# Attention scores on the four column quarters of the array, and VectorE to turn them back to pixels

## The chip, the cores and the metric

The kernel runs on one core of one Trainium2 chip. The metric is the device time of one execution in microseconds (us); the median over several runs counts. A core has TensorE (PE in the profile, with PEld for its weight loads), VectorE (DVE), ScalarE (ACT), GpSimd (POOL) and SyncE (SP), which run their own instruction streams and meet at semaphores. All data are fp32, and a fp32 matmul shows as two weight loads and two MATMUL instructions in the trace; a transpose by the identity shows as one of each.

## The reference

Two layers follow each other on x of shape (4, 64, 256, 256). The first is a transformer block with channel attention, a gated convolution and a patch-wise Fourier filter; the change does not touch it. The second, cut to what matters:

```python
def _lin_attn(x, wq, bq, wk, bk, wv, bv, wo, bo):      # x: (b, r, c, 64), 4 heads, one q and one k per head
    q = (x @ wq.T + bq).reshape(b_, r_, c_, H, DQK).swapaxes(2, 3)
    k = (x @ wk.T + bk).reshape(b_, r_, c_, H, DQK).swapaxes(2, 3)
    ...
    q = jax.nn.elu(q) + 1.0
    k = jax.nn.elu(k) + 1.0
    q = q / q.mean(axis=3, keepdims=True)
    k = k / k.sum(axis=3, keepdims=True)
    ktv = jnp.einsum('brhcd,brhce->brhde', k, v)
    o = jnp.einsum('brhcd,brhde->brhce', q, ktv)
    ...
xe = jnp.moveaxis(x, 1, -1)
h = xe + _lin_attn(_ln(xe, rn_g, rn_b), row_wq, row_bq, row_wk, ...)          # along rows
hc = _ln(h.swapaxes(1, 2), cn_g, cn_b)
h = h + _lin_attn(hc, col_wq, col_bq, col_wk, ...).swapaxes(1, 2)             # along columns
f = _ln(h, fn_g, fn_b)
f = jax.nn.gelu(f @ w1.T + b1, approximate=False) @ w2.T + b2
return jnp.moveaxis(h + f, -1, 1)
```

So each pixel has eight scores, four q and four k: a projection of its 64 channels by a 64x8 matrix, scaled by the pixel's reciprocal standard deviation, with a bias added.

## The kernel before

The program is a row of stages with HBM buffers between them. The first layer takes up to about 5390 us. **Stage c3** (to about 7300 us) ends the first layer (output projection and Fourier filter) and does the row attention of the second. **Stage d** (to the end) does the column attention and the feed-forward part. The change lies in these two.

**Stage c3** walks over 64 slabs: 2 pairs of images, 32 slabs of 8 rows each. Two images share a tile: 128 partitions by 16 blocks by 128 channels (two images of 64). Five generators work on different slabs at the same time, each one slab further behind: `product` (L938, output projection and transposes into zs), `patches` (L961, filter by matmuls L973 and L983, residual into xe at L986, layer-norm statistics), `features` (L1002), `attend` (L1039) and `update` (L1078). `_steps` calls them in turn, and each runs to its next `yield`.

`features` holds the projection. For each of four k, four blocks of xe are transposed on TensorE into one PSUM bank (L1009), ScalarE copies the bank to xrT (L1011), and four matmuls (L1014) project a block of 128 pixels each. The block is the stationary operand, 128x128, the weights rw (128x16, both images' 64x8 blocks) are the moving operand, and the result lies with pixels on partitions, 16 columns per block:

```python
for i in range(4):
    j = 4 * k + i
    T.matmul(qk[:, j * 16:(j + 1) * 16], xT[:, i * 128:(i + 1) * 128], rw, start=True, stop=True)
```

VectorE then scales (u, L1017), adds the bias (L1018), forms elu + 1 with ScalarE's Exp (`feature`, L672; f, L1021), and lays the scores out as kx (VectorE, L1028) and qx (GpSimd, L1029). `attend` multiplies kx into xe (L1046), `update` multiplies the mixed weights bdm into the pixels (L1085) and adds xe (h1, L1087).

**Stage d** walks over 32 iterations: 4 images, 8 groups of 32 columns. A tile h has 128 partitions (half of the 256 rows), 32 columns, two row halves and 64 channels. `attn` (L1157) of one group and `ffn` (L1248) of the group before it alternate through `_steps`. In `attn`, for each of 8 r, four columns are transposed (L1167), copied to xT by ScalarE (L1169) and projected by four matmuls (L1173) of the same form as L1014, with cwt in the place of rw; `spread` (L1139) takes the statistics of 16 channels' rows at a time. All 32 columns fill one bank qk of [128, 512]. Then u (L1176, L1177), fe, f (L1186) and kz (L1189) follow, and the products with h (L1195). `ffn` has the transposes L1255, the copy xfT (L1257), the first matmuls L1268, Gelu on ScalarE (L1270), and the second matmuls L1279 with the result st (L1281).

PSUM is split into six banks named mm and two named sm (`mm()` and `sm()`, L257 and L260). qk is an sm bank, and so are the products zp (c3) and the sums qs (d).

The source order gives the framework's scheduler a priority. The order of the instructions on each engine, and the buffers' turns, are planned by the scheduler with its own costs, so the order in the trace is not the order of the source.

Of the kernel before, what the change touches and what calls it, by code (L numbers as in the profile page):

```python
# [9 lines left out]
F32 = mybir.dt.float32  # L10
AF = mybir.ActivationFunctionType
ALU = mybir.AluOpType
# [235 lines left out]
def kernel(ctx: ExitStack, tc: tile.TileContext, x, packs, fd, out, off):  # L248
# [11 lines left out]
    def sm():  # L260
        return ps.tile([128, 512], F32, tag="sm", name="sm", bufs=2)
# [33 lines left out]
    def bc(ap, n):  # L295

        return ap.unsqueeze(2).to_broadcast([ap.shape[0], ap.shape[1], n])

    def mid_bc(ap, n):

        return ap.unsqueeze(1).to_broadcast([ap.shape[0], n, ap.shape[1]])
# [599 lines left out]
    def stage_c3():  # L901
        NS = H // 8
        with ExitStack() as cs:
# [3 lines left out]
            t = mm()  # L907
# [5 lines left out]

            t = mm()
            T.matmul(t[:, :16], K("rcen2"), rwg, start=True, stop=True)
            rw = p1.tile([128, 16], F32, name="rw")
            V.tensor_copy(rw, t[:, :16])
            t = mm()
            T.matmul(t[:65, :256], K("rcen1"), rgg, start=True, stop=True)
            rgt = p1.tile([65, 256], F32, name="rgt")  # L920
# [81 lines left out]
            def features(pr, s):  # L1002

                xe, rs = xes[pr, s]
                qk = sm()
                for k in range(4):
                    t = mm()
                    for i in range(4):
                        T.transpose(t[:, i * 128:(i + 1) * 128], xe[:, 4 * k + i], ident)  # L1009
                    xT = p.tile([128, 512], F32, name="xrT")  # L1010
                    S.copy(xT, t)  # L1011
                    for i in range(4):
                        j = 4 * k + i
                        T.matmul(qk[:, j * 16:(j + 1) * 16], xT[:, i * 128:(i + 1) * 128], rw, start=True, stop=True)  # L1014
                    yield
                u = p.tile([128, 32, 8], F32, name="u", bufs=1)
                V.tensor_tensor(u, qk[:, :256].rearrange("p (a c) -> p a c", c=8), bc(rs, 8), ALU.mult)  # L1017
                V.tensor_tensor(u, u, mid_bc(rbq, 32), ALU.add)  # L1018
                e = feature(p, u, [128, 32, 8])
                f = p.tile([128, 32, 8], F32, name="f", bufs=1)  # L1020
                V.scalar_tensor_tensor(f, u, 1.0, e, ALU.add, ALU.max)  # L1021

                qx = p.tile([128, 32, 8, 4], F32, name="qx")
                kx = p.tile([128, 32, 8, 4], F32, name="kx")
                mk = rmask.unsqueeze(1).unsqueeze(3)
                kr = p.tile([128, 32, 4], F32, name="kr", bufs=1)
                V.tensor_tensor(kr, f[:, :, 4:8], bc(rs, 4), ALU.mult)
                V.tensor_tensor(kx, kr.unsqueeze(2).to_broadcast([128, 32, 8, 4]), mk.to_broadcast([128, 32, 8, 4]), ALU.mult)  # L1028
                G.tensor_tensor(qx, f[:, :, 0:4].unsqueeze(2).to_broadcast([128, 32, 8, 4]), mk.to_broadcast([128, 32, 8, 4]), ALU.mult)  # L1029
                fr = p.tile([128, 2, 8], F32, name="fr")  # L1030
                V.tensor_reduce(fr, f.rearrange("p (j b) h -> p b h j", b=2), AX.X, ALU.add)
                qj = p.tile([128, 2, 2, 8, 4], F32, name="qj")
                kj = p.tile([128, 2, 8, 4], F32, name="kj")
                for b in (0, 1):
                    V.tensor_tensor(kj[:, b], mid_bc(fr[:, b, 4:8], 8), bc(rmask, 4), ALU.mult)
                    V.tensor_tensor(qj[:, :, b], fr[:, b, 0:4].unsqueeze(1).unsqueeze(1).to_broadcast([128, 2, 8, 4]), mk.to_broadcast([128, 2, 8, 4]), ALU.mult)
                fes[pr, s] = qx, kx, qj, kj
# [67 lines left out]
    def stage_d():  # L1105
        with ExitStack() as cs:
# [4 lines left out]

            t = mm()
            T.matmul(t[:, :16], K("cen2"), cwg, start=True, stop=True)
            cwt = p1.tile([128, 16], F32, name="cwt")
            V.tensor_copy(cwt, t[:, :16])
# [40 lines left out]

            def attn(h, xfs):  # L1157

                qk = sm()
                v1 = p1.tile([128, 64], F32, name="v1")  # L1160
                for r in range(8):
                    if r % 2 == 0:
# [5 lines left out]
                    xT = p.tile([128, 512], F32, name="xT")  # L1168
                    S.copy(xT, t)  # L1169
                    yield  # L1170
                    for i in range(4):
                        c = r * 4 + i
                        T.matmul(qk[:, c * 16:(c + 1) * 16], xT[:, i * 128:(i + 1) * 128], cwt, start=True, stop=True)  # L1173
                rs = rstd(v1, 64)
                u = p1.tile([128, 64, 8], F32, name="u")
                V.tensor_tensor(u, qk.rearrange("p (a c) -> p a c", c=8), bc(rs, 8), ALU.mult)  # L1176
                V.tensor_tensor(u, u, mid_bc(cbq, 64), ALU.add)  # L1177
                yield
                e = feature(p1, u, [128, 64, 8])
                yield  # L1180
                f = p1.tile([128, 2, 2, 32, 4], F32, name="f")
                uv = u.rearrange("p (c r) k -> p r c k", r=2)
                ev = e.rearrange("p (c r) k -> p r c k", r=2)
# [143 lines left out]
```

## Time and profile before

| | us |
|---|---|
| median of 3 runs (9669.94 to 9686.45) | 9681.12 |
| the profiled execution's own time | 9679.41 |
| span of the profile | 9677.6 |
| one slab of c3 (from L1051 to L1051) | 28.97 |
| one iteration of d (from L1210 to L1210) | 71.7 |

The profile is one execution. A row such as "L1014 PE MATMUL sm<-rw,xrT 128*128 128x16 f32 x2048 | 274.1, 266 | 12.7" says: line, engine, operation, output tile and inputs, the part of the array in use (rows*columns), the shape of the moving operand, the count, the busy time in us, the mean ns of one, and the idle time of the engine just before. Matmuls overlap, so 2048 of 266 ns make 274 us of busy time. In a timeline, the square bracket behind a row is the engine's idle time before it and what ended the idle time.

### The profile page before, as it was taken

How to read it: one execution, taken by the hardware profiler on the slowest of the kernel's cores; microseconds unless marked ns; L12 is line 12 of the kernel's file. 1: busy time of each engine (PE TensorE's matmuls, PEld its weight loads, DVE VectorE, ACT ScalarE, POOL GpSimd, SP SyncE). 2: the span in 40 equal slices, each digit the busy share in tenths (PEclk: the TensorE clock that was granted, in tenths of full speed). 3: DMA queues.
4: the chain of work that ended last, by engine and by line, in shares of the span. 5: the costliest groups of instructions: out<-in, count | busy, mean ns of one | idle time of the engine just before them, and what ended most of it. 6: DMA issues, size and time to landing. Idle time of an engine off the chain costs nothing. (4 is left out here: it accounts for less than half of the span.)

```text
span 9677.6 us, 130500 instructions
## 1 busy us (share of the span) xinstructions
PE 8860.6 (92%) x51310; PEld 4971.4 (51%) x51310; DVE 6090.5 (63%) x8570; ACT 4599.0 (48%) x7332; POOL 1134.1 (12%) x1828
## 2 busy tenths in 40 slices
PE   8999999698888888999999999999998999899997
PEld 7877777344444443333333466666665444444443
DVE  6666665466666664222222588888886777777775
ACT  4455555444444443222222344444444666666665
POOL 0111111111111111000000011111110000000000
PEclk9999999799999999999999999999997999999998
DMA  6677776799999998888888644444432322322322
GB/s 146 143 174 176 169 172 163 220 344 333 340 332 334 338 341 307 298 297 298 297 296 297 202 142 143 148 145 144 147 107 52 70 61 44 70 61 47 68 61 44
DMA packets 1258452, 1831.36 MB, mean 189 GB/s; under 512 B 335600, under 2 KB 1040112, under 8 KB 1196656
## 3 DMA queue, kind: packets, MB, share of 16 engines
q1 hardware_dynamic: 1053296, 1034.32, 36.7%
q0 software_dynamic: 204544, 788.69, 24.7%
q8 instruction: 407, 6.67, 0.3%
q14 instruction: 205, 1.68, 0.1%
HBM read 967.34 MB, written 788.53 MB: 181 GB/s over the span
## 5 line engine op out<-in xcount | busy, mean ns | idle before, releaser
L895 DVE TENSOR_TENSOR y<-ge,mm 128x512 f32<-128x512 f32 (+1 forms) x640 | 406.0, 635 | 1225.8 <-ACT ge L894 1225.8
L862 PE MATMUL mm<-t,w 128*128 128x512 f32 (+1 forms) x2560 | 1094.1, 566 | 19.6 <-DMA t<-td 19.6
L894 ACT ACTIVATE ge<-mm 128x512 f32<-128x512 f32 (+1 forms) x640 | 354.6, 554 | 1253.8 <-PE mm L869 1253.8
L862 PEld LDWEIGHTS mm<-t,w 128*128 128x128 f32 x2560 | 456.3, 190 | 647.3 <-issue 437.0
L755 PE MATMUL mm<-gp,wc 128*64 128x510 f32 (+1 forms) x3072 | 701.9, 596 | 83.1 <-DVE xm L765 50.9
L1270 ACT ACTIVATE hg<-mm,b 128x512 f32<-128x512 f32 x1024 | 629.3, 687 | 299.6 <-PE mm L1268 298.1
L599 PEld LDWEIGHTS mm<-wqk,gp 128*128 128x128 f32 x6144 | 712.0, 192 | 71.2 <-issue 42.3
L599 PE MATMUL mm<-wqk,gp 128*128 128x128 f32 x6144 | 733.7, 276 | 0.0
L1279 PE MATMUL mm<-hg,pack_d 128*64 128x512 f32 x2048 | 590.9, 632 | 109.7 <-ACT hg L1270 109.7
L810 ACT COPY tb<-mm 128x512 f32<-128x512 f32 x512 | 299.8, 586 | 779.8 <-PE mm L804 779.7
L804 PE MATMUL mm<-xl,pack_c 64*128 64x512 f32 x2048 | 532.5, 617 | 132.7 <-DVE tb L808 127.7
L1268 PE MATMUL mm<-xfT,w 64*128 64x512 f32 x2048 | 621.4, 673 | 3.2 <-ACT xfT L1257 2.9
L869 PE MATMUL mm<-t,w 64*64 64x504 f32 (+1 forms) x5120 | 575.6, 556 | 0.0
L755 PEld LDWEIGHTS mm<-gp,wc 128*64 128x64 f32 x3072 | 277.1, 137 | 462.3 <-issue 331.2
L309 ACT ACTIVATE ln_sq<-xn 128x1024 f32<-128x1024 f32 x256 | 274.6, 1073 | 429.0 <-DVE xn L307 428.9
L1281 DVE TENSOR_SCALAR st<-mm,pack_d 128x512 f32<-128x512 f32 x256 | 278.8, 1089 | 212.6 <-PE mm L1279 212.6
L804 PEld LDWEIGHTS mm<-xl,pack_c 64*128 64x128 f32 x2048 | 216.2, 189 | 376.7 <-DVE tb L808 186.7
L311 DVE TENSOR_REDUCE ln_v<-ln_sq 128x16 f32<-128x1024 f32 x256 | 311.6, 1218 | 146.8 <-ACT ln_sq L309 146.8
L765 DVE SCALAR_TENSOR_TENSOR xm<-mm,bx,xs 128x256 f32<-128x256 f32 x512 | 212.2, 476 | 297.3 <-PE mm L759 297.3
L1146 ACT ACTIVATE ln_sq<-xc 128x1024 f32<-128x1024 f32 x256 | 268.8, 1057 | 224.6 <-DVE xc L1144 223.4
L1268 PEld LDWEIGHTS mm<-xfT,w 64*128 64x128 f32 x2048 | 219.2, 206 | 297.6 <-issue 146.9
L1147 DVE TENSOR_REDUCE v<-ln_sq 128x16 f32<-128x1024 f32 x256 | 307.2, 1211 | 91.7 <-ACT ln_sq L1146 91.6
(448 smaller groups left out, 16826.0 us busy)
## 6 DMA issues: line engine op xcount, KB each, us to landing
t<-td SPq DMA_DIRECT2D x256, 1152.0 KB, 10.0
td<-tb POOLq DMA_DIRECT2D x144, 1024.0 KB, 10.6
td<-tb POOLq DMA_DIRECT2D x288, 512.0 KB, 9.2
yd<-y POOLq DMA_DIRECT2D x128, 1152.0 KB, 10.1
ya<-yd SPq DMA_DIRECT2D x192, 512.0 KB, 5.8
xs<-in_x_dram SPq DMA_DIRECT2D x128, 512.0 KB, 6.7
projd<-pj POOLq DMA_DIRECT2D x256, 256.0 KB, 4.8
gp<-projd SPq DMA_DIRECT2D x128, 512.0 KB, 7.5
```

The source lines that it names most:

```text
L311: V.tensor_reduce(s2, sq, AX.X, ALU.add)
L599: T.matmul(qp[:, k * 128:(k + 1) * 128], gp[:, 2 * i + k // 2, at + dx:at + dx + 128], wqk[:, dx, :], start=(dx == 0), stop=(dx == 2))
L755: T.matmul(tv[i * 64:(i + 1) * 64, :, o], wc[2 * pr + i][:, dx, :], gps[i][:, 2 * r:2 * r + 2, i_], start=(dx == 1), stop=False, skip_grou ...
L804: T.matmul(t, inT[q, hf * 128:(hf + 1) * 128], xls[b // 2, s][q, :, 2 * y:2 * y + 2].rearrange("p f y t -> p f (y t)"), start=True, stop=True)
L862: T.matmul(t[:, :n], w[:, 0:128], x_[:, c, :], start=True, stop=False, skip_group_check=True)
L869: T.matmul(t[po:po + 64, :n].rearrange("p (n c) -> p n c", c=64)[:, :, o], w[q:q + 64, 128:192], x_[q:q + 64, c, i_], start=False, stop=Tr ...
L894: S.activation(ge[:, :n], ts[0][k][:, :n], AF.Gelu)
L895: V.tensor_tensor(y[:, c, :].rearrange("p n c -> p (n c)"), ge[:, :n], ts[1][k][:, :n], ALU.mult)
L1147: V.tensor_reduce(s2, sq, AX.X, ALU.add)
L1268: T.matmul(t, w1[rh * 64:(rh + 1) * 64, i * 128:(i + 1) * 128], xT[rh * 64:(rh + 1) * 64], start=True, stop=True)
L1270: S.activation(g, t, AF.Gelu, bias=b1[:, i:i + 1])
L1279: T.matmul(y[rh * 64:(rh + 1) * 64, :], w2[:, i, :], hg[i * 2 + rh], start=False, stop=(i == 1), skip_group_check=True)
```

## The change

The operands are exchanged. The weights, filled up with zeros to 32 columns, become the stationary operand, 128x32, and the pixels become the moving operand. Of each of four blocks of 128 pixels, pixels 32g to 32g+31 go to column quarter g of the array: one matmul per quarter moves 4 x 32 = 128 pixels, and its result lies on partitions 32g to 32g+31, with the scores on partitions and pixels along the row. A group is still four matmul calls. VectorE then transposes the 32x32 blocks of a whole bank of [128, 512] into qp in SBUF, and so brings the pixels back to partitions, with 32 columns per block, of which 16 are used. In c3 the bank is filled once in a slab and transposed once. In d only 16 columns of the image fit into a bank, so there are two banks and two transposes per iteration, after r = 3 and r = 7. u reads the used columns of qp in place of qk. In c3 it writes to the tile u as before; in d it works in place in qp.

```diff
+    def bc4(ap, m, n):
+        v = ap.rearrange("p (a m) -> p a m", m=m)
+        return v.unsqueeze(3).to_broadcast([v.shape[0], v.shape[1], m, n])
...
-            rw = p1.tile([128, 16], F32, name="rw")
-            V.tensor_copy(rw, t[:, :16])
+            rw = p1.tile([128, 32], F32, name="rw")
+            V.memset(rw, 0.0)
+            V.tensor_copy(rw[:, :16], t[:, :16])
...
-                    for i in range(4):
-                        j = 4 * k + i
-                        T.matmul(qk[:, j * 16:(j + 1) * 16], xT[:, i * 128:(i + 1) * 128], rw, start=True, stop=True)
-                    yield
+                    for g in range(4):
+                        T.matmul(qk[g * 32:(g + 1) * 32, k * 128:(k + 1) * 128], rw, xT.rearrange("p (j n) -> p j n", j=4)[:, :, g * 32:(g + 1) * 32],
+                                 start=True, stop=True)
+                    yield
+                qp = p.tile([128, 16, 32], F32, name="qp")
+                V.transpose(qp.rearrange("p j m -> p (j m)"), qk)
                 u = p.tile([128, 32, 8], F32, name="u", bufs=1)
-                V.tensor_tensor(u, qk[:, :256].rearrange("p (a c) -> p a c", c=8), bc(rs, 8), ALU.mult)
+                V.tensor_tensor(u.rearrange("p (j b) c -> p j b c", b=2), qp[:, :, 0:16].rearrange("p j (b c) -> p j b c", b=2),
+                                bc4(rs, 2, 8), ALU.mult)
...
-                qk = sm()
+                qp = p1.tile([128, 32, 32], F32, name="qp")
...
                     yield
-                    for i in range(4):
-                        c = r * 4 + i
-                        T.matmul(qk[:, c * 16:(c + 1) * 16], xT[:, i * 128:(i + 1) * 128], cwt, start=True, stop=True)
+                    if r % 4 == 0:
+                        qk = sm()
+                    for g in range(4):
+                        T.matmul(qk[g * 32:(g + 1) * 32, r % 4 * 128:r % 4 * 128 + 128], cwt, xT.rearrange("p (c n) -> p c n", c=4)[:, :, g * 32:(g + 1) * 32],
+                                 start=True, stop=True)
+                    if r % 4 == 3:
+                        V.transpose(qp[:, r // 4 * 16:r // 4 * 16 + 16].rearrange("p c m -> p (c m)"), qk)
                 rs = rstd(v1, 64)
-                u = p1.tile([128, 64, 8], F32, name="u")
-                V.tensor_tensor(u, qk.rearrange("p (a c) -> p a c", c=8), bc(rs, 8), ALU.mult)
-                V.tensor_tensor(u, u, mid_bc(cbq, 64), ALU.add)
+                u = qp[:, :, 0:16].rearrange("p c (r k) -> p c r k", r=2)
+                V.tensor_tensor(u, u, bc4(rs, 2, 8), ALU.mult)
+                V.tensor_tensor(u, u, cbq.unsqueeze(1).unsqueeze(1).to_broadcast([128, 32, 2, 8]), ALU.add)
```

cwt is widened in the same way as rw, and the views of u and e behind it follow the new shape [128, 32, 2, 8].

More of the change, by code (lines that the diff above doesn't have):

```diff
@@ L1113, in stage_d @@
             T.matmul(t[:, :16], K("cen2"), cwg, start=True, stop=True)
-            cwt = p1.tile([128, 16], F32, name="cwt")
-            V.tensor_copy(cwt, t[:, :16])
+            cwt = p1.tile([128, 32], F32, name="cwt")
+            V.memset(cwt, 0.0)
+            V.tensor_copy(cwt[:, :16], t[:, :16])
             t = mm()
@@ L1170, in attn @@
                     yield
-                    for i in range(4):
-                        c = r * 4 + i
-                        T.matmul(qk[:, c * 16:(c + 1) * 16], xT[:, i * 128:(i + 1) * 128], cwt, start=True, stop=True)
+                    if r % 4 == 0:
[5 more added lines that the diff above has]
+                        V.transpose(qp[:, r // 4 * 16:r // 4 * 16 + 16].rearrange("p c m -> p (c m)"), qk)
                 rs = rstd(v1, 64)
-                u = p1.tile([128, 64, 8], F32, name="u")
-                V.tensor_tensor(u, qk.rearrange("p (a c) -> p a c", c=8), bc(rs, 8), ALU.mult)
-                V.tensor_tensor(u, u, mid_bc(cbq, 64), ALU.add)
+                u = qp[:, :, 0:16].rearrange("p c (r k) -> p c r k", r=2)
+                V.tensor_tensor(u, u, bc4(rs, 2, 8), ALU.mult)
+                V.tensor_tensor(u, u, cbq.unsqueeze(1).unsqueeze(1).to_broadcast([128, 32, 2, 8]), ALU.add)
                 yield
-                e = feature(p1, u, [128, 64, 8])
+                e = feature(p1, u, [128, 32, 2, 8])
                 yield
                 f = p1.tile([128, 2, 2, 32, 4], F32, name="f")
-                uv = u.rearrange("p (c r) k -> p r c k", r=2)
-                ev = e.rearrange("p (c r) k -> p r c k", r=2)
+                uv = u.rearrange("p c r k -> p r c k")
+                ev = e.rearrange("p c r k -> p r c k")
                 for rh in (0, 1):
```

## The prediction

> **What bounds the kernel now.** I read first the shares of busy time and the two stretches that the change touches (windows over the trace): stage c3, 5450 to 7270 us, and stage d, 7300 to 9670 us. Columns: stretch, us, then busy us and instructions of PE, PEld, DVE, ACT, POOL, granted TensorE clock, DMA share, GB/s.
>
> ```profile
> PE 8860.6 (92%) x51310; PEld 4971.4 (51%) x51310; DVE 6090.5 (63%) x8570; ACT 4599.0 (48%) x7332; POOL 1134.1 (12%) x1828
> 5450.00:7270.00 1820.00, 1715.15 (x10841) 1111.80 (x10840) 1506.65 (x2553) 810.78 (x1236) 266.10 (x373) 0.99 0.46 139
> 7300.00:9670.00 2370.00, 2113.67 (x11210) 1085.37 (x11210) 1723.38 (x2097) 1524.56 (x2206) 145.30 (x164) 0.92 0.27 58
> ```
>
> PE is busy 94% of c3 and 89% of d, but DVE has 83% and 73%, and ACT 64% in d. A saving on PE alone soon meets the next engine. Then the groups of PE by shape (busy us, mean ns of one):
>
> ```profile
> L1014 PE MATMUL sm<-rw,xrT 128*128 128x16 f32 x2048 | 274.1, 266 | 12.7 <-ACT xrT L1011 3.3
> L1173 PE MATMUL sm<-cwt,xT 128*128 128x16 f32 x2048 | 266.7, 265 | 11.1 <-ACT xT L1169 11.1
> L1195 PE MATMUL mm<-h,kz 128*32 128x512 f32 x512 | 63.3, 611 | 10.0 <-DVE kz L1189 10.0
> ```
>
> The two projections hold 541 us of PE, for 512 groups of four calls (a fp32 matmul shows as two instructions, so eight a group). L1195 is the form that replaces them: 128 rows by 32 columns of the array. Third, the timeline of one c3 slab (start us, us, engine, line, count, idle before it):
>
> ```profile
> 6018.98 1.07 PE L1014 MATMUL sm<-rw,xrT 128*128 128x16 f32 x8
> 6019.97 1.07 PE L946 MATMUL mm<-ya,pack_e 128*64 128x512 f32 x2
> ...
> 6022.10 0.69 DVE L977 TENSOR_TENSOR fs<-mm,fw 128x512 f32<-128x512 f32 x1 [2.31 <-PE mm L973]
> ...
> 6025.98 1.29 DVE L986 TENSOR_TENSOR xe<-mm,xmp 128x512 f32<-128x512 f32 x2 [2.20 <-PE mm L983]
> ...
> 6030.84 3.69 PE L1085 MATMUL mm<-bdm,qTr 128*128 128x256 f32 x16 [0.77 <-DVE bdm L1075]
> ...
> 6040.46 3.71 PE L1046 MATMUL sm<-xe,kx 128*64 128x128 f32 x32 [0.62 <-DVE kx L1028]
> ```
>
> A slab (29.0 us) has two halves. From 6011.5 (the L1046 before) to 6025.98 PE has no idle, and DVE waits 2.3 us for fs and 2.2 us for xe: **PE sets the time**. From 6025.98 to 6040.4 DVE has no idle at all (xe, m, s, xc, bdm, u, fs, sv, h, f, kr, kx) and PE waits 0.77 and 0.62 us for it: **DVE sets the time**. Fourth, an iteration of d:
>
> ```profile
> 8022.26 1.96 PE L1173 MATMUL sm<-cwt,xT 128*128 128x16 f32 x16 [0.37 <-ACT xT L1169]
> 8026.50 0.66 PE L1255 MATMUL mm<-pack_k,xf 128*128 128x128 f32 x4 [2.28 <-DVE xf L1245]
> ...
> 8037.20 2.55 PE L1279 MATMUL mm<-hg,pack_d 128*64 128x512 f32 x4 [1.96 <-ACT hg L1270]
> ...
> 8041.35 1.06 PE L1173 MATMUL sm<-cwt,xT 128*128 128x16 f32 x8
> ...
> 8065.18 1.92 PE L1195 MATMUL mm<-h,kz 128*32 128x512 f32 x16 [0.32 <-DVE kz L1189]
> ```
>
> Up to 8026.5 the chain of layer-norm operations on DVE sets the time, then ACT up to 8037.2; PE alone from there to about 8050 (ACT waits 3.2 us for the L1167 of 8049.35); then ACT works without a gap from 8050.1 to 8067.9 and ends in kz, for which PE waits; after that PE again, with no projection in it.
>
> [...]the 16 instructions of L1195 at 8065.18 are followed by the next line at 8067.03, so 1.85 us, where one 512-column instruction in single file takes 0.46 (L862, 128x512: 949.3 us for 2048): four run at a time. And a projection group runs 0.80 us from its first start to its last (1.07 less the last one's 0.27); the next line starts 0.11 us later where it is of the same 128*128 form (6027.73 to 6028.64) and 0.19 where it isn't (6018.98 to 6019.97): a switch costs 0.08.[...]
>
> **Part by part.** *PE, one group.* Old: 0.99 us to the next line (other form), 0.91 (same form, c3), 0.81 (same form, d, 8031.69 to 8032.50). New: two rounds of four tiles, 128 columns each, a quarter of 0.46 = 0.115, so 0.23, plus 0.03 for staggered starts and 0.09 for the switch out: 0.35. Where the line ahead was of the same form, 0.08 for the switch in, unless PE waits for the ACT copy there anyway. Bounds: 0.30, and 0.95 if the quarters did not overlap (no gain). I take 0.35, because L1195 shows the overlap for this very form.
> - c3, four groups a slab: two between other forms save 0.64 each, two between transposes about 0.5: 2.3 us, in 64 slabs 146 us.
> - d, eight an iteration: two at 0.64, one at 0.56, three at 0.38, the pair at 8022.26 about 1.2: 4.2 us, in 32 iterations 134 us.
>
> *Of that on the path.* c3: only the groups in the PE half, 6018.98 (0.64) and 6023.58 (0.56; the wait for xrT hides the switch in): 1.2 us. Those at 6027.73 and 6037.77 lie beside the DVE half and turn into longer waits for kx. d: 8041.35 (0.64), 8044.76 (0.38), 8048.44 (0.56): 1.58 us. The pair and the group at 8031.69 run into waits for xf and hg, the last two into ACT's stretch: nothing.
>
> *DVE, added.* 64 transposes of 128x512 in c3, two in each of 32 iterations of d. Nearest row: the DVE copy of 128x512 out of PSUM (L536), 681 ns.[...] Below 0.68 I exclude, since L536 already moves the same bytes without any reordering.[...] I take 0.71. In c3 the transpose must come after the last group (6027.73) and before u, inside the half that DVE sets: all 0.71 counts, and behind it queue u, fs, sv, h, kx; PE's L1046 waits for kx. In d the first (after r = 3, near 8042) falls where DVE waits 0.9 us for ln_sq; I charge 0.3. The second comes before u (8058.19); u and fe would end at 8060.5 to 8060.8, and ACT takes up the Exp only at 8061.72: nothing, unless ACT gets faster.
>
> *The rest.* u from SBUF with 16-element runs in place of PSUM: as L1018 and L1177 (417, 692 ns), no change. fe in d reads strided: 427 ns,[...] in the same cover of ACT, so nothing[...]. Two memsets, once. The sm buffers: one more turn per iteration in d, whose readers (transpose at r = 3, qr L684) are long done. No DMA is added or moved; SP and POOL are left alone.
>
> *Sum.* c3: 64 x (-1.2 + 0.71) = -31. d: 32 x (-1.58 + 0.3) = -41. From the profiled execution's 9679.4 us (span 9677.6; the median, 9681.1, is 0.02% higher) that gives 9607; I say 9608.
>
> What is unknown on both sides: the instruction order of each engine is planned anew (in the trace it isn't the source's: u stands ahead of sv). If the plan spread the saved PE time better, the whole 280 us less some new DVE waits is the floor. If it puts the transpose early, DVE stands at it with fs and h queued behind.
>
> **Rivals.**
> 1. *DVE becomes the bound of c3, and the clock falls with it: slower.*[...] 0.99 granted in c3, 0.92 in d, and eight L1268 take 3.38 us at 8027.88, just after the 2.28 us of idle, against 1.99 at 8049.91. The waits for kx would grow from 0.6 to 1.3 us or more (0.71 of transpose plus the group saved at 6037.77 makes about 2). If that halved one window in each slab, up to 1.7 us of work is lost: with a 1.24 us transpose, 64 x (-1.2 + 1.24 + 1.0) = +67, and d gaining little: near 9735. It decides once transpose and lost clock pass 1.2 us a slab.[...] Chance 0.20.
> 2. *The saving is hidden everywhere.* With 1.24 us a transpose and no loss of clock c3 comes out at 0 and d at -10 to -30, or the new plan costs as much: 9660 to 9700, about 9680. Chance 0.13.
> 3. *The plan rebalances.* c3 is then held by DVE's 24.3 us of work a slab (1506.65 over 62) and the added 0.7, at some 92% use, 27.2 us a slab, -110 in all; d saves 2 us an iteration, -64: 9505. For it: DVE's 4.5 us of waits in the PE half could take work. Chance 0.12.
> 4. *The quarters don't overlap* (group 0.95 us): +45 for transposes in c3, about 9730; L1195 speaks against it. It is inside rival 1's 0.20.
>
> **Numbers.** Forecast 9608, chance 0.55, its own spread 9560 to 9655. Range 9510 to 9725: it holds the forecast and rival 2 whole, and leaves out half of rival 3 (0.06) and somewhat over half of rival 1 (0.12). A difference of 0.2% (19 us) is about what a measurement of this kernel tells from none. Faster: 0.55 + 0.12 = 0.67; within it 0.13; slower 0.20.
>
> **What would show it.** The two projections as 128*32 128x128, 2048 instructions each, groups of eight 0.35 us apart from the next line, together some 170 us busy against 541. A DVE TRANSPOSE row, 128 times, near 0.71 us. In c3: slabs of 28.5 us, the wait for kx up from 0.6 to about 2 us, DVE's waits for fs and xe down by 1.2. In d: iterations of some 70.4 us against 71.7, waits for xf and hg longer. Wrong if the transpose takes over 1.2 us, if the granted clock of c3 falls under 0.96, or if the slab gets longer.

## The result, and the profile after

| | before | after |
|---|---|---|
| median, us (4 runs each, side by side) | 9681.65 (9669.94 to 9686.45) | 9594.86 (9592.56 to 9602.38) |
| span of the profile, us | 9677.6 | 9591.8 |
| c3, first to last slab mark | 1831.4 | 1860.1 |
| one slab of c3 | 28.97 (52 of 63) | 28.51 (20 of 63) or 30.18 (39 of 63) |
| d, first to last iteration mark | 2220.0 | 2119.9 |
| one iteration of d | 71.7 | 68.3 (six of 31 up to 69.1) |

The changed kernel takes 0.9913 of the time before (95% interval 0.9896 to 0.9931), 86.8 us less; 73 us less was forecast. The marks are the two reciprocals rz (L1051 and L1210 before, L1063 and L1231 after). The total hides an opposite pair: **c3 became longer by 28.7 us, d shorter by 100.1 us**. The remainder is at the edges: c3's first mark comes 6 us earlier, and the gap between the last mark of c3 and the first of d is 8.5 us shorter. So -6 + 28.7 - 8.5 - 100.1 = -86, the difference of the spans.

In the page after, the first line and the two stretches (windows; columns as before the change: us, then busy us and instructions of PE, PEld, DVE, ACT, POOL, granted clock, DMA share, GB/s):

```profile
PE 8630.7 (90%) x51310; PEld 4605.8 (48%) x51310; DVE 6148.5 (64%) x8700; ACT 4592.4 (48%) x7332; POOL 1140.4 (12%) x1828
5450.00:7290.00 1840.00, 1620.30 (x10794) 973.05 (x10794) 1523.83 (x2601) 806.45 (x1230) 268.41 (x369) 0.96 0.44 137
7310.00:9580.00 2270.00, 1981.71 (x11257) 881.62 (x11257) 1759.18 (x2177) 1517.66 (x2208) 147.06 (x168) 0.95 0.28 60
```

PE is busy 230 us less and DVE 58 us more (the transposes are 91 us, but kx takes 2.48 us in a slab in place of 2.85, medians). The number to notice is the granted clock: 0.99 became 0.96 in c3, and 0.92 became 0.95 in d. The clock records of the trace say it more closely. They list stretches at a granted clock of 0.50, here called half-clock windows. Of the 142 that begin in the two stretches named here, before and after, 120 last 3.413 us and the others two or three times that. They add up to 47.8 us before and 150.2 us after in c3 (5470 to 7290 us), and 249.2 and 118.0 us in d (7400 to 9480 us). The groups of the page:

```profile
L1021 PE MATMUL sm<-xrT,rw 128*32 128x128 f32 x2048 | 109.0, 285 | 12.5 <-ACT xrT L1018 3.2
L1190 PE MATMUL sm<-xT,cwt 128*32 128x128 f32 x2048 | 109.7, 287 | 13.8 <-ACT xT L1183 11.8
L1026 DVE STREAM_TRANSPOSE qp<-sm 128x512 f32<-128x512 f32 x64 | 45.4, 709 | 0.6 <-PE sm L1021 0.6
L1194 DVE STREAM_TRANSPOSE qp<-sm 128x512 f32<-128x512 f32 x64 | 45.2, 707 | 0.0
L680 DVE TENSOR_SCALAR fe<-qp 128x512 f32<-128x512 f32 x32 | 13.7, 427 | 1.1
```

The projections hold 219 us of PE in place of 541, and a transpose takes 0.71 us. fe reads strided in d and keeps its 427 ns. A slab of c3 in the timeline after (start us, us, engine, line, count, idle before it):

```profile
6024.61 0.43 PE L1021 MATMUL sm<-xrT,rw 128*32 128x128 f32 x8
6024.97 1.07 PE L953 MATMUL mm<-ya,pack_e 128*64 128x512 f32 x2
...
6027.09 0.69 DVE L984 TENSOR_TENSOR fs<-mm,fw 128x512 f32<-128x512 f32 x1 [1.48 <-PE mm L980]
...
6030.44 1.29 DVE L993 TENSOR_TENSOR xe<-mm,xmp 128x512 f32<-128x512 f32 x2 [1.73 <-PE mm L990]
...
6035.08 0.71 DVE L1026 STREAM_TRANSPOSE qp<-sm 128x512 f32<-128x512 f32 x1
6035.31 3.69 PE L1097 MATMUL mm<-bdm,qTr 128*128 128x256 f32 x16 [1.31 <-DVE bdm L1087]
...
6045.65 5.37 PE L1058 MATMUL sm<-xe,kx 128*64 128x128 f32 x32 [1.97 <-DVE kx L1040]
```

A group takes 0.36 us to the next line (6024.61 to 6024.97; 0.99 before). DVE's waits for fs and xe are shorter (2.31 and 2.20 before), and PE's wait for kx has grown from 0.62 to 1.97 us. The last line is the surprise: the same 32 instructions of the kx product took 3.71 us before. A window at half clock lies over them (granted clock, the third column from the end, 0.50; below it the same product before, at 1.00):

```profile
6046.83:6050.24 3.41, 3.41 (x19) 3.41 (x17) 2.88 (x3) 0.00 (x0) 0.00 (x0) 0.50 0.55 172
6040.46:6044.20 3.74, 3.74 (x33) 3.57 (x33) 3.67 (x8) 0.00 (x0) 0.50 (x1) 1.00 0.74 196
```

In d, the two PE waits of before that the prediction quotes now read:

```profile
8076.31 0.92 PE L1190 MATMUL sm<-xT,cwt 128*32 128x128 f32 x16 [0.37 <-ACT xT L1183]
8080.54 0.66 PE L1276 MATMUL mm<-pack_k,xf 128*128 128x128 f32 x4 [3.31 <-DVE xf L1266]
...
8087.11 2.36 PE L1300 MATMUL mm<-hg,pack_d 128*64 128x512 f32 x8
8089.40 0.66 PE L1181 MATMUL mm<-pack_k,h 128*128 128x128 f32 x4
```

The wait for xf is longer (2.28 before), and the second matmuls, L1300, run as eight without a wait; before they were split in four and four, and the second four waited 1.96 us for hg. A wait for hg now stands some 24 us later, where L1300 is split in two and six:

```profile
8110.81 2.23 PE L1300 MATMUL mm<-hg,pack_d 128*64 128x512 f32 x6 [1.55 <-ACT hg L1291]
```

### The profile page after: what moved, and what is told of

The parts are those of the page before. It is cut to its first block, busy times and chain, and to the rows that moved or that the text cites. A ratio compares the mean times of both kernels' runs of the same rounds, so it can differ in the third digit from the quotient of the medians.

```text
span 9591.8 us, 130417 instructions
## 1 busy us (share of the span) xinstructions
PE 8630.7 (90%) x51310; PEld 4605.8 (48%) x51310; DVE 6148.5 (64%) x8700; ACT 4592.4 (48%) x7332; POOL 1140.4 (12%) x1828
## 4 chain that ended last, share of the span: by engine, by line
PE 61%; DVE 18%; ACT 11%; DMA 6%; issue 3%; POOL 0%; SPq 0%; ACTq 0%; DVEq 0%; POOLq 0%
PE mm L867 11%; PE mm L874 6%; PE mm L1289 5%; PE mm L604 5%; PE mm L760 4%; DMA resp<-resd 4%; PE mm L1300 3%; PE sm L1058 3%; PE mm L1097 2%; PE sm L595 2%; PE mm L953 2%; ACT xl L797 2%; DVE kx L1040 2%; DVE ln_s L1156 2%; ACT ln_sq L314 1%
## 5 line engine op out<-in xcount | busy, mean ns | idle before, releaser
L1300 PE MATMUL mm<-hg,pack_d 128*64 128x512 f32 x2048 | 580.3, 609 | 100.2 <-ACT hg L1291 100.2
L1058 PE MATMUL sm<-xe,kx 128*64 128x128 f32 x2048 | 313.8, 327 | 135.9 <-DVE kx L1040 135.9
L953 PE MATMUL mm<-ya,pack_e 128*64 128x512 f32 x1024 | 381.3, 616 | 11.4 <-DMA ya<-yd 11.4
L1058 PEld LDWEIGHTS sm<-xe,kx 128*64 128x64 f32 x2048 | 298.3, 170 | 191.2 <-DVE kx L1040 187.7
```

The lines of the kernel that those rows point to most:

```text
L953: T.matmul(t[b * 64:(b + 1) * 64, :], owT, ya[:, :, 2 * r:2 * r + 2, b * 64:(b + 1) * 64].rearrange("p f y t -> p y f t"), start=True, sto ...
L1058: T.matmul(zp[:64, :128], kx[:, 2 * j:2 * j + 2].rearrange("p b y h -> p (b y h)"), xe[:, j, :], start=(j == 0), stop=(j == 15))
L1300: T.matmul(y[rh * 64:(rh + 1) * 64, :], w2[:, i, :], hg[i * 2 + rh], start=False, stop=(i == 1), skip_group_check=True)
```

## Experiments

Line numbers are those of each kernel. Ratios are to the kernel before on the same chip; a time without a ratio is one run.

| | time, us | ratio (95%) | c3 slab | d iteration |
|---|---|---|---|---|
| before | 9681.65 | 1 | 28.97 | 71.7 |
| after | 9594.86 | 0.9913 (0.9896 to 0.9931) | 28.51 / 30.18 | 68.3 |
| c3_only | 9700.65 | 1.0024 (1.0015 to 1.0033) | 28.5 / 30.2 | 71.7 |
| d_only | 9566.33 | 0.9883 (0.9866 to 0.9899) | 29.0 | 68.3 |
| c3_no_transpose | 9477.27 | | 27.8 | 68.3 |
| c3_two_transposes | 9673.71 | | 30.7 | 68.3 |
| fill_steps | 9578.6 | | steps | steps |
| c3_warm | 9529.03 | 0.9848 (0.9834 to 0.9863) | 28.5 | 68.3 |
| c3_moved | 9486.56 | | 27.87 | 68.3 |
| c3_mixed | 9422.85 | 0.9734 (0.9717 to 0.9750) | 26.74 | 68.3 |
| d_mixed | 9477.00 | 0.9796 (0.9780 to 0.9812) | 26.74 | 68.7 to 72.0 |
| d_old_warm_steps | 9742.98 | | 29.0 | steps |
| d_warm_steps | 9408.18 | | 26.74 | steps |
| d_warm8 | 9408.82 | 0.9725 (0.9708 to 0.9741) | 26.75 | 67.7 (22 of 31) |

### The parts alone: c3_only and d_only

c3_only has the changed c3 and stage d of before; d_only the reverse.

```diff
 # c3_only: stage d as before            # d_only: stage c3 as before
-                    for g in range(4):
-                        T.matmul(qk[g * 32:(g + 1) * 32, r % 4 * 128:...], cwt, xT...)
+                    for i in range(4):
+                        T.matmul(qk[:, c * 16:(c + 1) * 16], xT[:, i * 128:(i + 1) * 128], cwt, ...)
```

> Stage c3 of the changed kernel with stage d of the kernel before. If the two stages add up: c3 costs +29 us (64 slabs, from 1831 to 1860 us between the first and the last L1063), d keeps 71.7 us an iteration, so 9700 us in all (between 9690 and 9712), slower than before. Slabs of 28.5 us at full clock, and of 30.2 us where a half-clock window falls on the products with kx, two in three. Rival, the c3 loss comes from the stages' neighbourhood or from chance in the clock's phase: c3 within 10 us of before, 9672 to 9690 us.

> Stage c3 of the kernel before with stage d of the changed one. If the stages add up: d gains 100 us (iterations of 68.3 us against 71.7), so 9566 to 9582 us, faster than the changed kernel by 13 to 29 us. Rival, the gain of d hangs on where c3 leaves the clock's windows: iterations of another length, 69.5 to 71.7 us, and 9600 to 9680 us.

Measured: c3_only 1.0024, c3 1860.1 us as in the changed kernel, iterations 71.7; d_only 0.9883, slabs 29.0, d 2117.8 us. **The c3 part alone makes the kernel slower**, by 0.24% with an interval that leaves 1 out. **The d part alone comes out faster than both together** by the medians (9566 against 9595 us; the intervals of the two ratios just touch). Nearly all of the difference is in the stage that was changed, so each stage can be explained by itself.

### What the transpose costs c3: c3_no_transpose and c3_two_transposes

The first leaves the transposes of c3 out and lets u read the bank as it lies, so that each pixel gets the scores of others; the second adds one more, whose output nobody reads.

```diff
 # c3_no_transpose
-                V.transpose(qp.rearrange("p j m -> p (j m)"), qk)
-                V.tensor_tensor(u..., qp[:, :, 0:16]..., bc4(rs, 2, 8), ALU.mult)
+                V.tensor_tensor(u..., qk.rearrange("p (j m) -> p j m", m=32)[:, :, 0:16]..., bc4(rs, 2, 8), ALU.mult)
 # c3_two_transposes
+                qp2 = p.tile([128, 512], F32, name="qp2")
+                V.transpose(qp2, qk)
```

> The changed kernel without the transpose in c3: u reads the bank qk directly, so each pixel gets the scores of others; only the time is of interest. Theory, half of a slab is set by DVE and the transpose counts in full: a slab at full clock falls from 28.5 to 27.8 us (0.71 less; that is 1.2 less than the 28.97 before), PE's wait for kx from 1.97 to about 1.3 us, and fewer slabs have a half-clock window. Rival, the slab is set by PE and the clock alone: slabs stay at 28.5 and 30.2 us.

> The changed kernel with the bank transposed twice in c3, the second time into a buffer that nobody reads. Theory as above: a slab at full clock rises from 28.5 to 29.2 us, PE's wait for kx from 1.97 to about 2.7 us, and a half-clock window falls on the products with kx in nearly every slab (30.9 us). Rival, VectorE has room: slabs stay at 28.5 and 30.2 us.

Measured: slabs of 27.8 us (59 of 63) without, of 30.7 us (59 of 63) with two. Without the transpose the slab is 28.97 - 1.2 = 27.8: the two groups of the PE half bring what the prediction said they would. PE's wait for kx is about 1.3 us there, and hardly any half-clock window is left in c3 (17.1 us from the first to the last slab mark, against 160.4 in the changed kernel). The first transpose adds 0.71 us: 28.51. The second adds about 0.55: 30.7 less 1.67 for the half-clock window is 29.05, and the one slab that has no window shows 29.07. With two transposes the wait for kx is 2.51 us, and nearly every slab has the window (201.4 us at half clock in c3):

```profile
6005.53 0.72 DVE L1026 STREAM_TRANSPOSE qp<-sm 128x512 f32<-128x512 f32 x1
6006.16 0.69 DVE L1028 STREAM_TRANSPOSE qp<-sm 128x512 f32<-128x512 f32 x1
...
6016.69 5.38 PE L1060 MATMUL sm<-xe,kx 128*64 128x128 f32 x32 [2.51 <-DVE kx L1042]
```

### Is it the clock? fill_steps and c3_warm

Matmuls with a result that nobody reads (the fill) are put into c3 where PE waits, ahead of the kx product, and into d where it doesn't, behind the two transposes into qt: 0, 2, 4 or 8 of them in successive quarters of the stage, so that one run holds four sizes. In c3_warm, made later, c3 has four in every slab and d is left alone.

```diff
 # c3 (attend); c3_warm: fill = 4
+                fill = (0, 2, 4, 8)[(pr * 32 + s) // 16]
+                for _ in range(fill):
+                    T.matmul(zp[:, 128:256], ident, kr.rearrange("p a c -> p (a c)"), start=True, stop=True)
 # d (attn), fill_steps alone: by n // 8
+                if fill:
+                    tf = mm()
+                    for _ in range(fill):
+                        T.matmul(tf[:, :128], ident, fv[:, 0, 0], start=True, stop=True)
```

> The changed kernel with idle matmuls added, whose result nobody reads, in four equal parts of each stage. In c3 just ahead of the products with kx, in PE's wait: 0, 2, 4 and 8 matmuls of 128 columns (0, 0.43, 0.85, 1.7 us) for 16 slabs each. Theory, the 30.2 us slabs are the half clock after a wait of 2 us: from some size on all slabs take 28.5 us though PE does more; with 2 still some 30.2, with 8 all 28.5. Rival, the longer slabs come from a transfer or from DVE: 28.5 and 30.2 stay mixed, or 8 make slabs longer. In d behind the sums qs, where PE has no idle: 0, 2, 4 and 8 (0, 0.43, 0.85, 1.7 us) for 8 iterations each. If PE's time counts there one for one, iterations of 68.3, 68.7, 69.1 and 70.0 us. Rival, the iteration is held to whole or half clock windows (3.413 us x 20 = 68.27): it stays at 68.3 for the small ones and then jumps to 70.0 (20.5 windows) or 71.7 (21).

> The changed kernel with four idle matmuls (identity by kr, 128 columns) ahead of the kx products of every slab of c3; d untouched. Theory (the half-clock window is set off by the wait for kx, and is worth 1.67 us in two of three slabs): all slabs 28.51 us, no half clock on L1058's successor, half-clock time in c3 under 60 us instead of 150; c3 63 x 28.51 = 1796 to 1810 us instead of 1860, total 9541 us (9535 to 9555), ratio to before 0.9855. Rival (the three-slab pattern is a property of the schedule, and the steps of the earlier run only hit a favourable stretch): slabs mixed again, total 9580 to 9595.

Measured in c3: with no fill, slabs of 28.5 and 30.2 mixed; with two, four or eight matmuls 28.5 throughout, but for one of 31.6 where four become eight, and the last ones of the stage. A slab of fill_steps with two matmuls (the wait shown is what is left of it behind the fill):

```profile
6304.49 3.71 PE L1061 MATMUL sm<-xe,kx 128*64 128x128 f32 x32 [1.33 <-DVE kx L1040]
```

Two were enough already, against the expectation. Two matmuls that do nothing, which take 0.64 us out of a wait of 1.97 us, make the product behind them 3.71 us again and the slab 1.67 us shorter. The order of the instructions is not what did it: in the regular slabs DVE and ACT run the same sequence with two or four fill matmuls as without, and in the changed kernel the slabs of 28.51 and of 30.18 us have one and the same sequence on PE, DVE and ACT.

The clock records also show why only two slabs in three lose time. All half-clock windows in the regular slabs of the changed kernel begin on one grid of 3.413 us, to within 0.01 us. Columns as before (us, then PE's busy time first, granted clock third from the end); the first two rows and the next two are neighbours in the changed kernel, the last is of fill_steps with two matmuls:

```profile
6012.70:6016.12 3.42, 1.45 (x14) 0.66 (x7) 3.42 (x7) 0.43 (x1) 3.29 (x4) 1.00 0.43 108
6016.12:6019.53 3.41, 3.41 (x18) 3.41 (x17) 3.34 (x4) 0.00 (x0) 0.00 (x0) 0.50 0.70 198
6074.14:6077.55 3.41, 1.74 (x16) 1.74 (x17) 3.38 (x8) 0.00 (x0) 2.20 (x4) 1.00 0.55 144
6077.55:6080.96 3.41, 3.41 (x32) 3.21 (x30) 3.25 (x5) 0.30 (x1) 0.00 (x0) 1.00 0.43 129
6330.47:6333.88 3.41, 2.08 (x20) 1.39 (x13) 3.41 (x7) 0.20 (x1) 3.07 (x4) 1.00 0.43 108
```

Where the whole wait of 1.97 us falls inside one stretch of the grid, PE is busy for 42% of that stretch, and the next stretch is at half clock: so in 40 of 41 such slabs. Where a border of the grid splits the wait, PE is busy for more of either stretch (44% or more, but for one case within 0.02 us of a border, as the exception of the 41 is), and the next is at full clock: so in all 18. With two fill matmuls a stretch with the whole wait is busy for 61%. Three slabs, 88.87 us, are 26.04 stretches of the grid, so the pattern comes back after three.

c3_warm repeats the fill over the whole stage, here with four:

```profile
6055.65 3.71 PE L1061 MATMUL sm<-xe,kx 128*64 128x128 f32 x32 [0.88 <-DVE kx L1040]
```

59 of 63 slabs are 28.5 us, half-clock time is 41.0 us in place of 150.2 (24 of the 41 lie behind the last slab mark), c3 lasts 1792.4 us in place of 1860.1, and the whole is 9529.0 us, ratio 0.9848, an interval apart from that of the changed kernel. The rival, that the pattern belongs to the schedule, falls: its mixed slabs did not come back. **So the loss in c3 is the clock: 67.7 us of it.** With the fill c3 is 39 us shorter than before the change. Not all of that is the change: seven slabs of the kernel before take 30.0 or 30.6 us behind half-clock windows of their own, about 10 us in all, which are gone too. Slab against slab at full clock, 28.97 to 28.51, the change is worth 0.46 us, about 29 us over the stage, near the 31 forecast.

In d the fill did not help: iterations of 68.27, 69.15, 69.53 and 70.51 us on average for 0, 2, 4 and 8 fill matmuls, estimated at 0, 0.43, 0.85 and 1.7 us (two instructions each, and 0.108 us from one to the next in L1046 before). It costs what it lasts, plus about 0.45 us on average: the shortest iterations with two matmuls (68.72) are longer by little more than the 0.43, and in the others the half-clock window at xf lies earlier or is twice as long. At that place PE has no slack in d; the expected jumps to 70.0 or 71.7 did not come, so the idea that an iteration is tied to whole windows falls.

### A better mixture for c3: c3_moved and c3_mixed

In c3_mixed only the groups k = 1 and 2 have the new form, and k = 1 is issued one step later; k = 0 and 3 keep the old one, so the transpose has half the columns, and u is formed in two parts. c3_moved has the old form everywhere and only the later step, with stage d as changed.

```diff
 # c3_moved, from d_only
+                    if k == 1:
+                        yield
                     for i in range(4):
 ...
-                    yield
+                    if k != 1:
+                        yield
 # c3_mixed, from after
+                    if k in (1, 2):
+                        if k == 1:
+                            yield
+                            qq = mm()
+                        for g in range(4):
+                            T.matmul(qq[g * 32:(g + 1) * 32, (k - 1) * 128:k * 128], rw, xT...)
+                        if k == 2:
+                            V.transpose(qp.rearrange("p j m -> p (j m)"), qq[:, 0:256])
+                            yield
+                    else:
+                        ...                       # four matmuls of 16 columns, as before
```

> Stage d as changed; in c3 only the two groups of each slab that lie in the PE half (k = 1 and 2) go to the column quarters, into a bank of their own, and their 128x256 are transposed where VectorE waits for TensorE; k = 0 and 3 keep the old form. Theory, only those two groups are on the path, and only the transpose's place made it cost: a slab of 28.97 - 1.2 - 0.1 = 27.6 to 27.8 us, PE's wait for kx near 0.6 us as before the change, few half-clock windows, 9480 to 9500 us in all, faster than the changed kernel by 1.0 to 1.2%. Rival, all four groups count and the transpose costs wherever it stands: slabs of 28.5 to 29 us, 9545 to 9580.

> Control for c3_mixed: stage d as changed; c3 with the old form of the projection throughout, but with the group k = 1 issued one step later, as in c3_mixed, so that it comes behind the products L978 that VectorE waits for. c3_mixed took 26.74 us a slab, 0.9 less than the 27.6 expected. If that comes from the moved group: a slab of 28.97 - 0.9 = 28.0 us or less, about 9505 us in all. If the move is worth more, as the group now lies beside fs: down to 27.5. If it is worth nothing without the column quarters: 29.0 us, 9560 to 9570.

c3_mixed was forecast at 27.6 to 27.8 us a slab and came out at 26.74, since the later step had not been priced. c3_moved separates the two: 27.87 us, so of the 2.23 us a slab, 1.10 are the place of one group and 1.13 the new form on two groups. c3_mixed in the timeline:

```profile
6004.70 0.42 PE L1024 MATMUL mm<-xrT,rw 128*32 128x128 f32 x8
...
6006.94 0.45 DVE L1028 STREAM_TRANSPOSE qp<-mm 128x256 f32<-128x256 f32 x1 [0.52 <-PE mm L1024]
6008.31 1.29 DVE L993 TENSOR_TENSOR xe<-mm,xmp 128x512 f32<-128x512 f32 x2 [0.60 <-PE mm L990]
...
6013.17 3.69 PE L1108 MATMUL mm<-bdm,qTr 128*128 128x256 f32 x16 [0.77 <-DVE bdm L1098]
...
6022.74 3.71 PE L1069 MATMUL sm<-xe,kx 128*64 128x128 f32 x32 [0.57 <-DVE kx L1051]
```

The half transpose takes 0.45 us and now lies in what was a wait of DVE for PE; the waits for bdm and kx are 0.77 and 0.57 us, as before the change, and the kx product has its full clock. From 5500 to 7100 us PE is busy for 94% and DVE for 93%. This version is at 0.9734 faster than both kernels.

### Where d's gain comes from: d_mixed, d_old_warm_steps, d_warm_steps, d_warm8

d_mixed is c3_mixed with, in d, the new form for r = 2 to 5 only. The other three put idle matmuls ahead of the four transposes of xf, where PE waits: in the kernel before (d_old_warm_steps) and in c3_mixed (d_warm_steps), in four sizes over the iterations, and in every iteration (d_warm8).

```diff
 # d_mixed
+                    if 2 <= r < 6:
+                        T.matmul(qq[g * 32:(g + 1) * 32, (r - 2) * 128:(r - 1) * 128], cwt, xT...)   # for each g
+                        ...                       # one transpose after r = 5
+                    else:
+                        ...                       # as before, 16 columns
 # the other three, in ffn; d_warm8: fill = 8
+                    for _ in range(fill if r == 0 else 0):          # fill: (0, 4, 8, 12)[(n - 1) // 8]
+                        T.matmul(t[:, 0:128], ident, ident, start=True, stop=True)
```

> c3 as in c3_mixed (9423 us with the changed d); in d only r = 2 to 5 go to the column quarters and are transposed once, r = 0, 1, 6 and 7 keep the old form. Forecast of the path: only r = 3 to 5 lie where PE sets the time, so the iteration is 68.3 us or shorter by up to 0.7 (one transpose less), 9400 to 9425 us. Rival, all groups count, the saving of 3.4 us being spread over them: 69.5 to 70.5 us, 9460 to 9495 us.

> The kernel before, with idle 128-column matmuls in d ahead of the first transposes of xf, where PE waits 2.3 us for VectorE: 0, 4, 8 and 12 (0, 0.85, 1.7, 2.6 us) for 8 iterations each. Of the 3.4 us that an iteration of d lost, 1.3 were forecast from PE's time; the half-clock time in d fell from 8.0 us an iteration to 3.7, which is up to 2.1 us of work. If the clock made the rest: at some size the half-clock windows get fewer and iterations fall from 71.7 to between 69.6 and 70.8 us, though PE does more. Rival, the rest comes from another order of the instructions: 71.7 us or more at every size.

> The same idle matmuls in d of the kernel c3_mixed, whose d is that of the changed kernel: 0, 4, 8 and 12 for 8 iterations each. There PE waits 3.3 us for xf and one half-clock window follows in each iteration, on matmuls that ScalarE's Gelu doesn't wait for long. If that window costs nothing: 68.3 us for all sizes, or a little more where the fill spills over. If it is on the path: 66.6 to 67.5 us at some size.

> c3_mixed with eight idle matmuls ahead of the four xf transposes in every iteration of d. Theory (the one window left in an iteration is set off by the wait for xf, and costs 0.6 us net): iterations 67.7 us instead of 68.3, half-clock time in d under 40 us, c3 as in c3_mixed (26.74); total 9423 - 32 x 0.6 = 9404 us, ratio to before 0.9714. Rival (the size that suited one quarter of the iterations drifts with the phase of the windows): iterations between 67.7 and 69, total 9404 to 9430, no gain.

Measured: **d_mixed** missed its forecast and loses to c3_mixed (9477.0 against 9422.9 us), and shows why. Its wait of 1.96 us for hg is back, and the clock records show three kinds of iteration, later in a cycle of five: 68.72 us with one half-clock window, nearly always of 6.8 us (at the wait for xf), 71.95 us with a second of 6.8 us behind the wait for hg, and 70.22 us where that second one lasts 3.4 us. So a half-clock window at this second place costs 3.23 us for 6.8 us, 1.50 us for 3.4 us. The mean, 69.98 us, lies where the rival of the expectation put it; but the iterations without the second window, at 68.72, are within 0.43 us of the full change, so most of the excess is the clock and not the groups left in the old form.

```profile
8000.20 2.54 PE L1316 MATMUL mm<-hg,pack_d 128*64 128x512 f32 x4 [1.96 <-ACT hg L1307]
8002.67 2.07 PE L1305 MATMUL mm<-xfT,w 64*128 64x512 f32 x2
8004.68 0.65 PE L1200 MATMUL sm<-xT,cwt 128*32 128x128 f32 x8
8005.26 3.14 PE L1305 MATMUL mm<-xfT,w 64*128 64x512 f32 x6
```

Before the change the same place has one window in each iteration. Its timeline, where the L1279 behind the wait and the first L1268 fall into the window and the L1279 ahead of it and the later L1268 do not, and the window itself:

```profile
8033.57 1.08 PE L1279 MATMUL mm<-hg,pack_d 128*64 128x512 f32 x4
...
8037.20 2.55 PE L1279 MATMUL mm<-hg,pack_d 128*64 128x512 f32 x4 [1.96 <-ACT hg L1270]
8039.67 1.75 PE L1268 MATMUL mm<-xfT,w 64*128 64x512 f32 x2
...
8042.35 1.98 PE L1268 MATMUL mm<-xfT,w 64*128 64x512 f32 x6
8037.56:8040.97 3.41, 3.41 (x6) 0.79 (x4) 3.41 (x4) 2.65 (x5) 0.00 (x0) 0.50 0.00 0
```

In the changed kernel the eight L1300 come without that wait, and its iterations have a single window, at the wait for xf (3.4 us, in four of 31 iterations 6.8).

What this window costs in the order of before can be read from c3_only, whose stage d runs the same sequence on PE, DVE and ACT as the kernel before. Its second to fifth iteration have the wait for hg and no window behind it, and take 70.23 us; from the sixth on the window is there and they take 71.63 to 71.72 us. So there it costs 1.4 to 1.5 us, as in d_mixed. In the same four iterations the window at xf lasts 3.4 us once and 6.8 us three times, and the time is the same. One of the four, to be compared with 2.55 and 1.75 above:

```profile
7554.26 1.65 PE L1291 MATMUL mm<-hg,pack_d 128*64 128x512 f32 x4 [1.96 <-ACT hg L1282]
7555.84 1.12 PE L1280 MATMUL mm<-xfT,w 64*128 64x512 f32 x2
```

Why the wait is gone from this place shows on ACT, first before and then after the change:

```profile
8032.25 1.27 ACT L1270 ACTIVATE hg<-mm,b 128x512 f32<-128x512 f32 x2
8033.53 1.28 ACT L1152 ACT_TABLE_LOAD   x1
8034.83 0.32 ACT L1152 ACTIVATE ln_d<-v,eps_t 128x32 f32<-128x32 f32 x1
8035.17 1.28 ACT L1270 ACT_TABLE_LOAD   x1
8036.46 1.26 ACT L1270 ACTIVATE hg<-mm,b 128x512 f32<-128x512 f32 x2
...
8084.04 0.69 ACT L1291 ACTIVATE hg<-mm,b 128x512 f32<-128x512 f32 x1
8084.62 1.99 ACT L1160 ACTIVATE ln_sq<-xc 128x1024 f32<-128x1024 f32 x2
8086.52 1.83 ACT L1291 ACTIVATE hg<-mm,b 128x512 f32<-128x512 f32 x3
```

Before, the square root ln_d (0.32 us) and two table loads (1.28 us each) stood between the two halves of hg; the new plan puts them behind hg here. (Another ln_d, the one ahead of u, now stands in the middle of a later hg, where the wait of 1.55 us is.) In d_mixed the plan puts ln_d between the two halves again.

**d_old_warm_steps** missed its expectation: iterations of 71.7 us with no fill and of 72.2 to 75.2 (one 77.8) with it, although half-clock time fell from 249 to 184 us. But the fill also made the plan put another projection group ahead of xf, so its order is not that of the kernel before, and the run itself says nothing on the window.

**d_warm_steps** has 68.3 us with no fill, with four 67.7 where no half-clock window is left (four of eight iterations) and 68.5 to 69.5 in the others, 67.71 with eight (no half-clock window at all), 68.7 with twelve (no window either). Here too the fill makes the plan put another projection group ahead of xf, so 68.3 against 67.7 compares two orders.

**d_warm8** has one order in all its regular iterations: 22 of 31 iterations have no window and take 67.7 us; in eight a window of 3.4 us came back at the wait for xf, as the rival had it, and they take 68.3 to 68.4. So a window at this place costs 0.6 to 0.7 us, not 1.7. Half-clock time in d is 59 us, not under 40, and d takes 2104.1 us against 2117.4. In the total (9408.8 us, 0.9725) the 14 us from c3_mixed are less than the two intervals tell apart. With d_warm_steps (9408.2 us, one run) it is the fastest of the kernels tried, by that little.

## Why the prediction came out right

The time lies 13 us under the forecast, and that is luck. The steps on PE and DVE held; but the sums for the two stages were off by much, in opposite directions, c3's by the clock and d's by the clock and a new order on ACT.

- **What bounds a slab and what a group costs: right.** 0.36 us a group against 0.35, 128*32 tiles overlapping as in L1195, whose 16 instructions of 512 columns took 1.85 us; DVE waits less for fs and xe by 1.3 us a slab (totals of the waits, 5470 to 7290 us: 277.3 to 194.8, over 63 slabs) against 1.2. The rival that the quarters don't overlap is out.
- **The transpose: right in size and place.** 709 ns against 0.71 us. That was the author's estimate, and the 1.24 us of the rivals a supposed upper case; the rows of before show a floor alone, the 681 ns of the copy L536. With the 450 ns of a 128x256 in c3_mixed a column costs 1.01 ns, near the 1.06 between u's two rows before (420 ns for 128x256, 692 for 128x512). All of it is on the path in c3, as c3_no_transpose shows (27.8 against 28.51 us). The wait for kx: 1.97 us against "about 2".
- **c3 in sum: wrong.** Forecast -31, measured +28.7. At full clock the slab is 28.51, the 28.5 of the forecast. The term that failed is "64 x (-1.2 + 0.71)", which has no loss of clock in it; the clock took 67.7 us. Rival 1 had it: a wait for kx near 2 us, then one halved window, "up to 1.7 us of work". It came so, 1.67 us, in two slabs of three, without the 1.24 us transpose that rival 1 put beside it. By the prediction's own signs c3 was wrong as well: the slab got longer (29.5 us on average against 29.1), and the granted clock fell to 0.96.
- **The clock behind the old groups.** Before the change each of the seven slabs of 30.0 or 30.6 us has a half-clock window behind a stretch of 3.413 us in which PE was busy for 75 or 82% and which holds a whole group of the 16-column form and a short wait (0.77 us for bdm or 0.62 for kx). That these groups set the windows off is not shown: 25 other stretches with such a group, busy for 75 to 82%, had full clock behind them. In the regular slabs after the change no stretch busy for more than 42% had a window behind it; those with the whole wait of 1.97 us, at 42%, did (granted clock 0.50 over 3.41 us, 1.00 with two fill matmuls in the wait).
- **d in sum: mis-sized.** Forecast -1.28 us an iteration, measured -3.4. What was missed is again a window: the 3.4 us at half clock behind the wait for hg were taken as given, and went with the wait, since the new plan moved ln_d on ACT. c3_only prices the window at 1.4 to 1.5 us in the order of before. That the plan would move ln_d was not foreseen, so this part is luck. The rest, 70.23 to 68.29 us, each with a window at xf, is 1.94 us against 1.28. These 0.7 us more are not divided by any run: the wait for hg itself, gone from its place, and the first transpose, charged with 0.3, may hold them. The length of the window at xf does not, in the order of before (70.23 us with 3.4 and with 6.8).
- **ACT's cover, fe, u: right as far as seen.** fe takes 427 ns; the wait for xf is longer by 1.0 us, as said. The wait for hg was to grow too; at the place quoted it is gone, and one of 1.55 us stands later.
- **Busy time of the projections: 219 us against some 170.** It is the union of overlapping instructions (0.43 us for a group of which 0.36 counts to the next line); it is not on the path, the 0.36 us is.
- The -6 and -8.5 us at the stage edges were not in the sum; their cause stays open.

The forecast was saved by cancellation: c3 came out 60 us above its forecast and d 59 us below, and -14 fell at the edges. The condition of rival 1, over 1.2 us a slab, was met (0.71 of transpose and 1.67 x 2/3 of clock are 1.8), and c3 by itself makes the kernel slower, as c3_only shows; what rival 1 had wrong was that d would gain little.

## What to carry to other kernels

When a change moves work from TensorE to another engine, look at the wait that this makes TensorE stand in: here, where a wait of 1.97 us left PE busy for 42% of a stretch of 3.413 us, the matmuls behind it ran at a granted clock of 0.50 in 40 of 41 slabs. The price was that of the half-clock window and not of the wait: 1.67 us for 3.4 us at half clock behind kx, 1.4 to 1.5 behind hg, 0.6 to 0.7 behind xf. Whether the wait was hit changed with where the grid of the windows fell on it (two slabs of three), so compare iterations with and without a window inside one run; that prices it without a new kernel. Two matmuls of no use, which took 0.64 us out of that wait, or only as much of the change as kept the wait short (two groups of four, 0.57 us), won it back. And compare the granted clock stage by stage on both sides (here 0.99 to 0.96 in c3, 0.92 to 0.95 in d), for a total that looks right may hold two errors.

## What the runs showed of the hardware that was not expected

- Two fill matmuls in a wait of 1.97 us kept the clock full in 16 slabs, four of them did so over the whole stage (67.7 us). The cost of a window of 3.4 us differed by its place: 1.67 us behind the wait for kx, 1.4 to 1.5 behind the wait for hg, 0.6 to 0.7 behind the wait for xf in d_warm8.
- The half-clock windows in the regular c3 slabs of the changed kernel begin on one fixed grid of 3.413 us. A wait of 1.97 us inside one stretch of it (PE busy 42%) was followed by half clock in the next in 40 of 41 slabs, the same wait across a border in none of 18. That made slabs of 28.5 and 30.2 us in a pattern of three, so a loop with one order of instructions showed two times.
- Four quarters of 128x32, 128 columns each, take 0.36 us for a group of four fp32 calls, where the 16-column form took 0.81 to 0.99 for the same result.
- VectorE's transpose of 32x32 blocks, fp32 out of PSUM: 709 ns for 128x512, 450 ns for 128x256.
